# TensorE multiplies the identity until the first rows come, and turns W itself in place of loading its transpose

## The chip, the cores and the metric

The kernel runs on one core of one Trainium2 chip. The metric is the device time of one launch in microseconds (us). One profiled execution is shown beside the timed runs: its span (first to last instruction) and its own time are given below. Engines are named as in the profile: PE is TensorE's matmul, PEld its weight load, DVE VectorE, ACT ScalarE, POOL GpSimd, SP SyncE, which issues most transfers.

## What is computed

A perceiver block in float32: cross-attention of 8 x 64 rows of `x` over 1601 context rows per batch, a linear-attention block with a feed-forward part, and a mixture of 8 experts. Only the first stage concerns the change:

```python
# x: (8, 64, 512), context: (8, 1601, 512), W: (512, 512), b: (512)
p       = layernorm(x)                        # rows of the queries
trans_q = einsum('bqh,oh->bqo', context, W) + b
scores  = einsum('bph,bqh->bpq', p, trans_q)
att     = softmax(scores)
vec     = einsum('bpq,bqh->bph', att, context)
x       = x + relu(einsum('bph,oh->bpo', vec, W) + b)
# then the linear attention with its feed-forward part, then the experts
```

`W` is used twice. The kernel multiplies `W` into the 512 rows of `p` rather than into the context, which contracts over `W`'s first axis; the output projection contracts over its second axis and so needs `W` transposed.

## The kernel before

Every engine's instructions run in the order in which the source writes them. The 512 rows are four tiles of 128 (`t` = 0 to 3, two batches each), and the 512 channels are four blocks of 128 (`KC`).

*Head.* SP issues the loads of `x` (L101, two transfers) and of `W` (L113, tile `w_sb`). GpSimd clears five stretches of `v_sb` (L122) into which the bias row and the last context rows will be loaded, then builds the identity (`make_identity`), then `eps` and further constants. VectorE and ScalarE compute the layer norm of two tiles at a time (L352 to L363). TensorE transposes each tile (`turn_p`, L370) by products with the identity, ScalarE copies the result to `p_t` (tile `h_t`, L371), and `pw_half` (L380) multiplies `W` into it: two halves of 256 rows, four channel blocks each. The order is rows 0 and 1, two blocks of the first half, rows 2 and 3, the rest. ScalarE copies each result to `pw_t` (L387). VectorE then spreads the bias over the partitions (L407) and forms `pb` (L411), which ScalarE adds to the scores as it copies them (L450).

*Cross-attention.* `key_group(t, g)` multiplies `pw_t` by a quarter of the transposed context of two batches (L442, two tiles `ctxT` of 0.8 MB). `softmax` and `turn_scores` (L475) follow, and `weigh(t, g)` (L503) multiplies the weights by the context rows (two tiles `ctx` of 1 MB for each of three groups). `turn_av` and `attended` (L530, L537) apply the output projection with `w_t`, the transposed `W`. These steps are interleaved over the tiles: the key groups of tile 0, two of tile 1, and then in each round one tile's weighing with the next tiles' key groups.

*Transfers.* `stream` writes down one list of loads, and `issue_to` issues them on SP in that order. Context tiles and later weights share a ring of twelve tiles (`RING`); an issue waits until the oldest tile in it has been given back by `done`. The transposed `W` stands in this list behind the first row group of tile 0 (`xw_t`, L197), outside the ring. Each issue also waits for the transfer eight places earlier.

*PSUM.* There are two kinds of banks with four buffers each, `mm` and `acc`. Transposes and the product with `W` use `mm`; scores, weighted sums and outputs use `acc`.

After the cross-attention come the linear attention (from 127 us on), the feed-forward part and the experts (from about 410 us), which the change does not touch.

Of the kernel before, what the change touches and what calls it, by code (L numbers as in the profile page):

```python
# [20 lines left out]
P = 128  # L21
# [3 lines left out]
KC = D // P  # L25
# [15 lines left out]
NBIG = 7  # L41
LN_EPS = 1e-5
RING = 12
AHEAD = 6


@with_exitstack
def perceiver_kernel(
# [5 lines left out]
    context_tail: bass.AP,  # L54
    context_last: bass.AP,
    xw: bass.AP,
    xw_t: bass.AP,
    xb: bass.AP,
    wq: bass.AP,
    wk: bass.AP,  # L60
# [11 lines left out]
    nc = tc.nc  # L72
    const = ctx.enter_context(tc.tile_pool(name="const", bufs=1))
    resid = ctx.enter_context(tc.tile_pool(name="resid", bufs=1))
    ring = ctx.enter_context(tc.tile_pool(name="ring", bufs=RING))
    tails = ctx.enter_context(tc.tile_pool(name="tails", bufs=2))
# [7 lines left out]
    def mm_bank(name):  # L84
        return ps.tile([P, 512], F32, tag="mm", name=name)
# [26 lines left out]
    w_sb = xa.tile([P, KC, D], F32, tag="w", name="w_sb")  # L112
    nc.sync.dma_start(w_sb, xw)  # L113
    w_t = xa.tile([P, KC, D], F32, name="w_t")
# [3 lines left out]
    half = H * DH // 2  # L118
    last_in = [v_sb[:, 2, :half], v_sb[:, 2, half:], v_sb[:, 3, half:], v_sb[:, 1, half:]]
    xb_in = v_sb[:, 0, :D]  # L120
    for rows in [xb_in, *last_in]:
        nc.gpsimd.memset(rows, 0.0)  # L122
    col = const.tile([P, COLS], F32, name="col")

    streamed, order, issued = {}, [], [0]
# [2 lines left out]
    def stream(key, src):  # L128
        order.append((key, src))

    def stream_keys(t, g):
        if t < NT:
            for h in range(2):
                src = context_t[2 * t + h, D * SW * g : D * (SW * g + WIDTHS[g])]
                stream(("ctxT", t, g, h), src.rearrange("(p c k) -> p c k", p=P, c=KC))

    def stream_rows(t, g):
        for h in range(2):
            src = context[2 * t + h, g * GK : (g + 1) * GK, :]
            stream(("ctx", t, g, h), src.rearrange("(p c) d -> p c d", c=GK // P))  # L140
# [9 lines left out]
        stream_keys(1, g)  # L150
    for t in range(NT):
        stream_rows(t, 0)
        if t == 0:
            stream("xw_t", xw_t)
        stream_keys(t + 1, 2)
        stream_rows(t, 1)
        stream_keys(t + 1, 3)
        stream_rows(t, 2)
        stream(("tail", t), context_tail[t])
        for g in range(2):  # L160
            stream_keys(t + 2, g)
        if t == NT - 2:
            for n in range(2):
                stream(("wv", n), wv[n])
# [13 lines left out]
                stream(("e_wo", e, q // 2), e_wo[e, q // 2])  # L178
    place = {key: i for i, (key, _) in enumerate(order)}

    places_of = {"xb": xb_in[0:P:32, :], "col": col, "xw_t": w_t}
    places_of.update({("last", t): last_in[t][0:P:32, :] for t in range(NT)})

    def in_ring(key):
        return key[0] not in places_of and key not in places_of and key[0] != "tail"

    def issue_to(n):

        while issued[0] < min(n, len(order)):
            key, src = order[issued[0]]  # L190
            if in_ring(key) and len(held) >= RING:
                if held[0] not in freed:
                    return
                held.pop(0)
            if key in places_of:
                t_ = places_of[key]
                nc.sync.dma_start(t_, src)  # L197
            elif key[0] == "tail":
                t_ = tails.tile([P, D], F32, tag="tail", name="_".join(str(k) for k in key))
                nc.sync.dma_start(t_, src)  # L200
            else:
                width = WIDTHS[key[2]] if key[0] == "ctxT" else 512
                t_ = ring.tile([P, 4, width], F32, tag="ring", name="_".join(str(k) for k in key))
                nc.sync.dma_start(t_, src)
                held.append(key)
            streamed[key] = t_
            issued[0] += 1

    def done(*keys):

        freed.update(keys)

    def need(*key):
        if key[0] not in ("ctxT", "ctx", "tail", "wv"):
            done(*[k for k in held if place[k] < place[key] - AHEAD + 1])
            issue_to(place[key] + 1 + AHEAD)
        else:
# [3 lines left out]

    ident = const.tile([P, P], F32, name="ident")
    make_identity(nc, ident)
    eps = const.tile([P, 1], F32, name="eps")
    nc.gpsimd.memset(eps, LN_EPS)
    warm0 = const.tile([P, 1], F32, name="warm0")
# [123 lines left out]
    def statistics(src, name):  # L350
        st = small.tile([P, 6], F32, tag="st", name=f"st_{name}")
        nc.vector.bn_stats(st, src)  # L352
        mv = small.tile([P, 2], F32, tag="mv1", name=f"mv_{name}")
        nc.vector.bn_aggr(mv, st)
        std = small.tile([P, 1], F32, tag="std1", name=f"std_{name}")
        nc.scalar.activation(std, mv[:, 1:2], AF.Sqrt, bias=eps)
        return mv, std

    def normalize(dst, src, mv, std, name):

        rstd = small.tile([P, 1], F32, tag="rstd1", name=f"rstd_{name}")
        nc.vector.reciprocal(rstd, std)
        nc.vector.tensor_scalar(dst, src, mv[:, 0:1], rstd, ALU.subtract, ALU.mult)  # L363
# [3 lines left out]
    def turn_p(t):  # L367
        bank = mm_bank(f"tr_p_{t}")
        for c in range(KC):
            nc.tensor.transpose(bank[:, c * P : (c + 1) * P], pn[:, t, c * P : (c + 1) * P], ident)  # L370
        nc.scalar.copy(p_t[:, :, t * P : (t + 1) * P], bank.rearrange("p (c q) -> p c q", c=KC))  # L371
# [4 lines left out]
    def pw_half(half, hc):  # L376
        cols = slice(half * 2 * P, (half + 1) * 2 * P)
        bank = mm_bank(f"pw_{half}_{hc}")
        for oc in range(KC):
            nc.tensor.matmul(  # L380
                bank[:, : 2 * P],
                w_sb[:, oc, hc * P : (hc + 1) * P],
                p_t[:, oc, cols],
                start=(oc == 0),
                stop=(oc == KC - 1),
            )
        nc.scalar.copy(pw_t[:, hc, cols], bank[:, : 2 * P])  # L387
# [3 lines left out]
    for t in range(0, NT, 2):  # L391
        of = [statistics(xs[:, t + h, :], f"p_{t + h}") for h in range(2)]
        for h in range(2):
            normalize(pn[:, t + h, :], xs[:, t + h, :], *of[h], f"p_{t + h}")
        if t == 0:
            turn_p(0)
            turn_p(1)
    pw_half(0, 0)
    pw_half(0, 1)
    turn_p(2)  # L400
    turn_p(3)
    pw_half(0, 2)
# [652 lines left out]
    t = NT - 1  # L1055
# [583 lines left out]
    "ctx_tail",  # L1639
    "ctx_last",  # L1640
    "L0_xattn_W",
    "L0_xattn_W_T",
    "L0_xattn_b",
    "L0_attn_wq",
    "L0_attn_wk",
# [82 lines left out]
```

## Time and profile before

| | us |
|---|---|
| median of 3 timed runs | 650.71 (650.0 to 650.8) |
| the profiled execution, its own time | 647.66 |
| its span | 645.5 |
| TensorE busy in the span | 620.4 (96%) |
| first transpose of rows starts | 7.45 |
| first product with W starts | 10.06 |
| first scores product starts | 27.95 |
| load of the transposed W issued | 31.75 |
| first use of the transposed W | 70.8 |

The page shows the span in 40 slices of 16.1 us; a digit is a busy share in tenths. In the chain of waits, a line holds the start, the duration and what the end of the span was waiting for at that time. In a timeline, a line holds start, duration, engine, source line, operation, output and inputs, the shape and the count; in brackets stand the idle time before it and what ended it. In a table by stretches, the columns are the stretch, its length, the busy time and count of PE, PEld, DVE, ACT and POOL, then granted clock, share of the transfer engines, and GB/s.

### The profile page before, as it was taken

Reading aid. Unit: us, or ns where it says so; the run is one execution under the profiler, and the core shown is the slowest. Engines: PE = TensorE matmul, PEld = TensorE weight load, DVE = VectorE, ACT = ScalarE, POOL = GpSimd, SP = SyncE. Lnnn points to the kernel's source line nnn. Section 1 sums busy time; section 2 is a strip of 40 time slices with the busy share of each in tenths; the row PEclk is TensorE's granted clock in tenths of the full one; section 3 lists DMA queues with packets and bytes.
Section 4 is the critical chain, followed back from the end, with each engine's and each line's share of the span. In section 5 each row is a group of like instructions: output and inputs, shape, how many; then the busy total and the mean of one; then the engine's idle time right before and its main releaser. Section 6 shows DMA issues by size and latency. Waiting matters only on the chain.

```text
span 645.5 us, 7558 instructions
## 1 busy us (share of the span) xinstructions
PE 620.4 (96%) x2956; PEld 292.7 (45%) x2956; DVE 185.5 (29%) x450; ACT 127.8 (20%) x245; POOL 64.6 (10%) x87
## 2 busy tenths in 40 slices
PE   4999999999999999999999999999999999999994
PEld 3743434344444444455444447544443344444441
DVE  5011333332316888660000035511311211011100
ACT  2241222220132123031101211311111111111110
POOL 4000000000000000050000002250102012103000
PEclk9999999999999999999999999999999999999998
DMA  8999999999421203030312222339392549496611
GB/s 345 405 414 422 423 425 421 427 426 422 193 80 47 86 2 131 1 131 0 130 52 79 70 96 95 134 95 348 114 375 54 200 206 338 173 367 188 274 18 16
DMA packets 23755, 132.70 MB, mean 206 GB/s; under 512 B 4084, under 2 KB 4084, under 8 KB 12184
## 3 DMA queue, kind: packets, MB, share of 16 engines
q1 hardware_dynamic: 19352, 123.37, 48.0%
q0 software_dynamic: 3248, 7.58, 5.3%
q10 hardware_dynamic: 1104, 1.07, 0.5%
q8 instruction: 33, 0.54, 0.3%
q14 instruction: 18, 0.15, 0.1%
HBM read 127.10 MB, written 4.91 MB: 204 GB/s over the span
## 4 chain that ended last, share of the span: by engine, by line
PE 50%; DMA 23%; issue 22%; DVE 2%; POOL 1%; POOLq 1%; ACT 0%; SPq 0%; ACTq 0%
DMA out_dram<-y_sb,dst_late 11%; DMA ctx<-in_ctx_dram 11%; PE hid L839 8%; PE mlp L860 8%; PE wk L647 4%; PE wq L647 4%; PE v L567 4%; PE wo L758 4%; PE sc L442 3%; PE av L503 3%; PE pw L380 3%; PE pr_wq L663 1%; PE xo L537 1%; PE qk L689 1%; POOL xg L1166 1%
## 5 line engine op out<-in xcount | busy, mean ns | idle before, releaser
L1243 PE MATMUL up<-e_up,xgT 128*128 128x512 f32 x224 | 100.2, 595 | 2.3 <-PEq L1569 1.4
L1243 PEld LDWEIGHTS up<-e_up,xgT 128*128 128x128 f32 x224 | 40.9, 190 | 49.9 <-issue 48.1
L1251 PE MATMUL y<-e_wo,hidT 128*128 128x512 f32 x128 | 60.8, 598 | 0.0
L839 PE MATMUL hid<-v_sb,w 128*128 128x512 f32 (+2 forms) x144 | 56.6, 545 | 0.0
L1202 DVE TENSOR_TENSOR mid<-up,act 128x256 f32<-128x256 f32 x35 | 14.9, 425 | 132.0 <-ACT act L1200 132.0
L860 PE MATMUL mlp<-w,hid_sb 128*128 128x512 f32 x112 | 51.0, 597 | 0.0
L503 PE MATMUL av<-ctx,eT 128*64 128x512 f32 x192 | 46.6, 597 | 0.7 <-DMA ctx<-in_ctx_dram 0.6
L442 PE MATMUL sc<-ctxT,pw_t 128*64 128x401 f32 (+1 forms) x256 | 46.2, 501 | 0.0
L839 PEld LDWEIGHTS hid<-v_sb,w 128*128 128x128 f32 x144 | 26.2, 190 | 29.1 <-issue 27.3
L1224 POOL DMA_INDIRECT out_dram<-y_sb,dst_late x12 | 18.3, 1524 | 174.3 <-ACT y_sb L1223 55.7
L1200 ACT ACTIVATE act<-up 128x256 f32<-128x256 f32 x35 | 13.4, 384 | 107.2 <-PE up L1243 97.4
L854 POOL TENSOR_TENSOR xin<-xin,b_bc 128x512 f32<-128x512 f32 x4 | 5.1, 1265 | 272.6 <-DVE rstd_h L796 268.4
L1251 PEld LDWEIGHTS y<-e_wo,hidT 128*128 128x128 f32 x128 | 22.5, 190 | 19.9 <-issue 19.6
L860 PEld LDWEIGHTS mlp<-w,hid_sb 128*128 128x128 f32 x112 | 20.7, 190 | 23.5 <-issue 23.4
L442 PEld LDWEIGHTS sc<-ctxT,pw_t 128*64 128x64 f32 x256 | 19.5, 136 | 25.6 <-issue 24.3
L758 PE MATMUL wo<-wo,a_t 128*128 128x512 f32 x64 | 29.1, 600 | 0.5 <-DVE a_t L734 0.5
L647 PE MATMUL wk<-h_t,wk 128*128 128x512 f32 x64 | 29.5, 604 | 0.0
L647 PE MATMUL wq<-h_t,wq 128*128 128x512 f32 x64 | 29.4, 602 | 0.0
L567 PE MATMUL v<-wv,h_t 128*128 128x512 f32 x64 | 28.7, 596 | 0.6 <-DVE h_t L554 0.6
L908 DVE TENSOR_TENSOR xs<-mlp,xs 128x512 f32<-128x512 f32 x3 | 2.1, 692 | 86.6 <-PE mlp L860 86.6
L732 DVE RECIPROCAL rden<-rden 128x512 f32<-128x512 f32 x8 | 26.8, 3353 | 0.3
L503 PEld LDWEIGHTS av<-ctx,eT 128*64 128x64 f32 x192 | 13.7, 136 | 26.8 <-issue 23.2
(266 smaller groups left out, 651.4 us busy)
## 6 DMA issues: line engine op xcount, KB each, us to landing
e_up<-in_L_ffn_up_dram SPq DMA_DIRECT2D x32, 1024.0 KB, 8.0
ctx<-in_ctx_dram SPq DMA_DIRECT2D x24, 1024.0 KB, 17.2
ctxT<-in_ctx_T_dram SPq DMA_DIRECT2D x24, 802.0 KB, 14.8
e_wo<-in_L_ffn_wo_dram SPq DMA_DIRECT2D x16, 1024.0 KB, 9.6
w<-in_L_attn_w_dram SPq DMA_DIRECT2D x8, 1024.0 KB, 4.7
ctxT<-in_ctx_T_dram SPq DMA_DIRECT2D x8, 796.0 KB, 17.5
wv<-in_L_attn_wv_dram SPq DMA_DIRECT2D x2, 1024.0 KB, 16.6
wq<-in_L_attn_wq_dram SPq DMA_DIRECT2D x2, 1024.0 KB, 17.8
```

The source lines that it names most:

```text
L380: nc.tensor.matmul(bank[:, : 2 * P], w_sb[:, oc, hc * P : (hc + 1) * P], p_t[:, oc, cols], start=(oc == 0), stop=(oc == KC - 1),)
L442: nc.tensor.matmul(sc[h * S : (h + 1) * S, :width], pw_t[:, c, (2 * t + h) * S : (2 * t + h + 1) * S], keys[h][:, c, :], start=(c == 0), s ...
L503: nc.tensor.matmul(av[h * S : (h + 1) * S, :], e_t[:, 4 * g + j, h * S : (h + 1) * S], rows[h][:, j, :], start=(g == 0 and j == 0), stop=F ...
L567: nc.tensor.matmul(bank, h_t[:, c, t * P : (t + 1) * P], wv_n[:, c, :], start=(c == 0), stop=(c == KC - 1))
L647: nc.tensor.matmul(bank, w[:, c, (j % 4) * P : (j % 4 + 1) * P], h_t[:, c, :], start=(c == 0), stop=(c == KC - 1),)
L732: nc.vector.reciprocal(rden, rden)
L758: nc.tensor.matmul(wo_banks[t], a_t[:, j, t * P : (t + 1) * P], wo_r[j // 4][:, j % 4, :], start=(j == 0), stop=(j == nj - 1),)
L839: nc.tensor.matmul(hid_banks[f][:, tokens], w[:, c, (f % 4) * P : (f % 4 + 1) * P], h2_t[:, c, tokens], start=(c == 0), stop=(c == KC - 1),)
L860: nc.tensor.matmul(acc[t], hid[:, t * P : (t + 1) * P], need("w2", f // 4)[:, f % 4, :], start=(f == 0), stop=(f == FF // P - 1),)
L1224: nc.gpsimd.indirect_dma_start(out=out, out_offset=bass.IndirectOffsetOnAxis(ap=dst[:n, :], axis=0), in_=y_sb[:n, :], in_offset=None, boun ...
L1243: nc.tensor.matmul(bank, xg_t[c], up_of[q][:, c, :], start=(c == 0), stop=(c == KC - 1))
L1251: nc.tensor.matmul(y, h_t[:, j, :], w[:, 2 * (q % 2) + j, :], start=(q + j == 0), stop=(q + j == NQ))
```

## The change

Twelve products of the identity with itself are written on TensorE right behind the making of the identity, into a bank that nothing reads; the five clears of GpSimd move behind the identity. The load of the transposed `W` and its input go. In its place TensorE transposes the sixteen 128 x 128 blocks of `w_sb` between the transposes of rows 0 and 1 and the product with `W`, into four `acc` banks, and VectorE copies these to `w_t` behind the layer norm of the rows.

```diff
+NIDLE = 12
...
-    for rows in [xb_in, *last_in]:
-        nc.gpsimd.memset(rows, 0.0)
...
     for t in range(NT):
         stream_rows(t, 0)
-        if t == 0:
-            stream("xw_t", xw_t)
         stream_keys(t + 1, 2)
...
     ident = const.tile([P, P], F32, name="ident")
     make_identity(nc, ident)
+
+    idle_bank = acc_bank("idle")
+    for _ in range(NIDLE):
+        nc.tensor.matmul(idle_bank[:, :P], ident, ident, start=True, stop=True)
+    for rows in [xb_in, *last_in]:
+        nc.gpsimd.memset(rows, 0.0)
     eps = const.tile([P, 1], F32, name="eps")
...
         if t == 0:
             turn_p(0)
             turn_p(1)
+
+            w_banks = [acc_bank(f"w_t_{hc}") for hc in range(KC)]
+            for hc in range(KC):
+                for oc in range(KC):
+                    nc.tensor.transpose(
+                        w_banks[hc][:, oc * P : (oc + 1) * P], w_sb[:, oc, hc * P : (hc + 1) * P], ident
+                    )
     pw_half(0, 0)
     pw_half(0, 1)
+    for hc in range(KC):
+        nc.vector.tensor_copy(w_t[:, hc, :], w_banks[hc])
     turn_p(2)
     turn_p(3)
...
-    inputs["L0_xattn_W_T"] = _np.asarray(inputs["L0_xattn_W"]).T
```

## The prediction

> **What bounds the kernel now.** I read the page's busy rows and slices first, then the chain of waits, then the first 180 us engine by engine.
>
> ```profile
> PE 620.4 (96%) x2956; PEld 292.7 (45%) x2956; DVE 185.5 (29%) x450; ACT 127.8 (20%) x245; POOL 64.6 (10%) x87
> PE   4999999999999999999999999999999999999994
> DMA  8999999999421203030312222339392549496611
> ```
>
> TensorE works from the first slice to the last. In the first ten slices (0 to 161 us, the cross-attention) the transfers are at their limit too, at some 0.42 MB per us. Both engines are full there, so one must ask which is late at each place. The chain in order of time says it:
>
> ```profile
> 7.45 1.95 PE tr_p L370 x8
> ...
> 10.06 6.72 PE pw L380 x16
> 16.78 0.87 PE tr_p L370 x8
> 17.65 10.36 PE pw L380 x48
> 28.02 13.68 PE sc L442 x80
> ...
> 42.09 17.31 DMA ctx<-in_ctx_dram
> ```
>
> To 42 us it is TensorE. Then three times (59.40, 87.9/90.3 and 121.2 us) it goes through the landing of a context tile. TensorE's own timeline gives the size of these three waits. The first sixteen products of the third row group of token tile 0 need 4.80 us; without a wait they need 3.65 us:
>
> ```profile
> 58.29 4.80 PE L503 MATMUL av<-ctx,eT 128*64 128x512 f32 x16
> 76.00 3.65 PE L503 MATMUL av<-ctx,eT 128*64 128x512 f32 x16
> 90.34 3.65 PE L503 MATMUL av<-ctx,eT 128*64 128x512 f32 x14 [0.29 <-DMA ctx<-in_ctx_dram]
> 121.25 3.65 PE L503 MATMUL av<-ctx,eT 128*64 128x512 f32 x14 [0.29 <-DMA ctx<-in_ctx_dram]
> ```
>
> The first wait is 4.80 - 3.65 = 1.15 us. At the other two, two records starting at 89.03 and 119.94 us need 0.45 us and the next ones start 1.31 us later: 0.85 us each (part of it is booked as busy). Together TensorE waits 2.85 us for transfers before 121.25 us. After that no single wait of TensorE is over 1.0 us to the end of the span, and none is for a transfer: what is gained at 121.25 us stays.
>
> The two sides are tied at one place. The ring of twelve tiles is full at 25.8 us, and the next transfer is issued only when the first scores product has given its tiles back, at 30.89 us. By then the transfers have nearly run dry:
>
> ```profile
> 30.89 0.80 SPq L204 DMA_DIRECT2D ctx<-in_ctx_dram  x2
> 31.00:32.00 1.00, 1.00 (x8) 0.43 (x6) 0.00 (x0) 0.54 (x1) 0.00 (x0) 1.00 1.14 376
> 32.00:33.00 1.00, 1.00 (x8) 0.43 (x6) 0.00 (x0) 0.00 (x0) 0.00 (x0) 1.00 0.84 232
> ```
>
> The last column is GB/s, about 420 elsewhere: (44 + 188 + 14) / 420 = 0.6 us of transfer time are lost from 31 to 34 us.
>
> **The change, part by part.** *The load of W's transpose goes.* It is 1024 KB at 31.75 us, ahead of all but two of the context's row tiles: 1.049 MB / 0.422 MB per us = 2.48 us. Every later landing comes that much earlier if SP issues in time.
>
> *The first products at half speed.* Sixteen records of the W product take 6.72 us, forty-eight take 10.36: 0.427 us from start to start against 0.216. The starts change pace at 15.9 us. (The profile's granted-clock column says 1.00 throughout; only the starts show it.) So 10.06 to 15.9 us costs 5.84 / 2 = 2.9 us. Thirty-two products in the code give 64 records, while a transpose gives one. The twelve products of the identity are hence 24 records of 128 columns. A transpose of that width starts every 0.214 us at half speed (eight in 1.95 us with a wait between, five in 1.30) and every 0.109 at full speed (eight in 0.87); a record of a product has the same rate per column (256 columns 0.427). They run 24 x 0.214 = 5.1 us.
>
> *When they can start.* Before, GpSimd clears five tiles first (2.37 us) and the identity is ready at 3.70 us. Moved ahead, it is ready near 1.37 us, so TensorE works from about 1.45 to 6.6 us, ends 0.85 us ahead of the first normalized rows (7.45 us), and delays nothing. The clears now end at 3.8 us. Behind them on GpSimd stands eps, needed by ScalarE's square root at 5.91 us; on SP the bias load (3.61 us) may wait 0.3 us, and the key loads behind it come while 3.7 MB are under way. No cost.
>
> *The sixteen transposes of W*, between the transposes of the rows and the W product. At full speed: rows 0 to 7.9 us, rows 1 from 8.05 (normalized at 8.02) to 8.5, W landed at 1.74 + 7.1 = 8.84, so 16 x 0.109 = 1.74 takes them to 10.6. ScalarE's two copies (0.59 each) end at 9.2 beneath them, and the gap of 0.68 us that TensorE had is filled. Then 16 x 0.216 = 3.45, 0.87, 48 x 0.216 = 10.36: the scores start at 25.3 us in place of 28.0, TensorE 2.7 us ahead. At half speed: 16 x 0.214 = 3.43, and the W product starts at 12.6 us.
>
> *Four copies of 512 columns out of PSUM on VectorE*: nearest row, the copy of avT at 0.69 us; 2.8 us, from 11.7 to about 14.5. Behind them on VectorE stand the bias shuffle and pb (3.3 us), done near 18.5 instead of 15.9; the first reader is ScalarE's scores copy, at 28 us or later. The scores reuse the banks, free at 14.5. w_t is first read at 70.8 us. No cost, as long as the scores don't start before 18.5.
>
> *Does the pace rise?* The row: it rose at 15.9 us, 5.8 us after the first product and 8.4 us after the first transpose. [...]
>
> **The sum.** If TensorE is 0.6 us or more ahead at the first scores, the dip at 31 to 34 us goes as well, and the landings move by 2.48 + 0.6 = 3.1 us. TensorE itself could move by 2.85 + 2.7 = 5.5 us. The smaller counts: 3.1 us at 121.25 us, and I take 3.0. From the profiled span: 645.5 - 3.0 = 642.5 us, its own time 647.66 - 3.0 = 644.7. The shown runs lie 3 us above the profiled one; the difference carries over: 650.7 - 3.0 = 647.7 us. Note what the sum says: most of TensorE's lead comes back as longer waits for context, and the removed load is worth more than the faster clock.
>
> **The rivals.** [...]
>
> *The load was hidden anyway.* Then only TensorE's lead would count and the waits at the three places would not shrink or move; gain 0 to 0.4, time 650.5. Against it: the transfers are full from 4 to 166 us and three waits end in a landing.
>
> *The head turns into the bound (slower).* One mechanism: W's transposes at half speed push the W product to 12.6 us, and full speed comes late. Break-even is where half the slow time equals 0.38 + 2.48, that is full speed at 18.3 us; from 20.9 us on it is slower by more than 1.3 us. At 23 us the scores start 4.8 us late, the transfers stand idle meanwhile, and the time is 650.7 + 4.8 - 2.5 = 653.0. Against it: no stretch of the trace is slow for more than 8.4 us after TensorE's start.
>
> **How the numbers follow.** Forecast 0.70 (its own range 646.8 to 648.6), pace stays low 0.18, load hidden 0.05, head as bound 0.07. 0.2% of the time, 1.3 us, is about what a measurement of this kernel can tell from no change. Faster: 0.70 and a little of the second, 0.72; same: the rest of the second and the third, 0.21; slower 0.07. Likeliest 647.7; the range reaches from 646.6 (a lead that also spares the small dips at 23 to 25 us, and the runs' spread of 0.4) to 650.5, well into the second case.
>
> **What would show it.** W-product starts 0.216 us apart from the first; identity records from 1.5 to 6.6 us; first scores near 25.3 us; no dip at 31 to 34 us; the landing at 121.25 us now near 118.2, with TensorE's three waits no shorter than before. Wrong would be: starts 0.427 us apart after 12.6 us, scores later than 28 us, or landings at 59.4, 90.3 and 121.2 us that have not moved.

## The result and the profile after

The changed kernel takes 648.17 us (median of 11 runs, 646.47 to 649.68) beside 650.62 us before (11 runs). The ratio is 0.9955, 95% interval 0.9941 to 0.9969: faster by 0.45%, 2.9 us (2.0 to 3.8); the two medians lie 2.45 us apart. Five of the eleven runs took 646.5 to 647.4 us at a mean granted clock of 0.996, and six took 648.2 to 649.7 us at 0.993; the profiled execution (span 645.1 us, own time 646.8 us) is one of the five.

Busy rows and slices of the page, after:

```profile
PE 623.1 (97%) x2996; PEld 296.0 (46%) x2996; DVE 187.7 (29%) x454; ACT 128.0 (20%) x245; POOL 64.6 (10%) x87
PE   8999999999999999999999999999999999998994
DMA  8999999999411103030311323249382749497511
```

TensorE has 40 records more (24 products of the identity, 16 transposes) and is busy in the first slice. The rest looks as before, which is why the head must be read instruction by instruction. TensorE's timeline after:

```profile
1.45 4.55 PE L223 MATMUL idle<-ident 128*128 128x128 f32 x24 [1.45 <-POOL ident masks.py:199]
7.25 1.38 PE L372 MATMUL tr_p<-ident,xin 128*128 128x128 f32 x8 [1.25 <-DVE xin L365]
8.91 1.96 PE L404 MATMUL w_t<-ident,w_sb 128*128 128x128 f32 x16 [0.29 <-DMA w_sb<-in_L_xattn_W_dram]
10.71 3.62 PE L382 MATMUL pw<-h_t,w_sb 128*128 128x256 f32 x16
...
57.23 3.65 PE L514 MATMUL av<-ctx,eT 128*64 128x512 f32 x14 [0.37 <-DMA ctx<-in_ctx_dram]
88.26 3.65 PE L514 MATMUL av<-ctx,eT 128*64 128x512 f32 x14 [0.38 <-DMA ctx<-in_ctx_dram]
119.12 3.65 PE L514 MATMUL av<-ctx,eT 128*64 128x512 f32 x14 [0.25 <-DMA ctx<-in_ctx_dram]
```

The 24 records need 4.55 us where 5.1 was worked out for half speed throughout; their starts change pace at about 4.8 us. The first sixteen records with W need 3.62 us in place of 6.72. The three waits for context are still there, 2.2, 2.1 and 2.1 us earlier than before (59.44, 90.34, 121.25).

The head in the chain of waits after, where the load of W has become its first link:

```profile
1.74 7.12 DMA w_sb<-in_L_xattn_W_dram
...
8.91 1.96 PE w_t L404 x16
10.87 3.46 PE pw L382 x16
14.33 0.87 PE tr_p L372 x8
15.21 10.36 PE pw L382 x48
25.57 10.98 PE sc L453 x64
...
36.94 15.38 DMA ctxT<-in_ctx_T_dram
```

TensorE reaches the scores 2.45 us earlier (25.50 in place of 27.95), and from 36.5 us on the chain follows transfers; before, it left TensorE only at 41.7 us. The dip of 31 to 34 us is gone, but a longer one has come. By stretches of a microsecond, last column GB/s, after:

```profile
23.00:24.00 1.00, 1.00 (x6) 0.87 (x6) 0.00 (x0) 0.12 (x1) 0.00 (x0) 1.00 1.02 351
...
26.00:27.00 1.00, 1.00 (x10) 0.42 (x8) 0.00 (x0) 0.00 (x0) 0.00 (x0) 1.00 0.94 309
...
28.00:29.00 1.00, 1.00 (x10) 0.42 (x8) 0.00 (x0) 0.51 (x1) 0.00 (x0) 1.00 1.00 263
...
31.00:32.00 1.00, 1.00 (x10) 0.42 (x8) 0.00 (x0) 0.60 (x1) 0.00 (x0) 1.00 1.01 411
```

Against 420, the eight stretches from 23 to 31 us (351, 352, 367, 309, 385, 263, 359, 391) lack 583 KB, 1.4 us of transfer time. The share of the transfer engines stays at 0.94 to 1.03 in these stretches, so they are not idle; their packets take longer, and the profile does not say why. The kernel before lost 0.3 us at 23 to 25 (377 and 329 GB/s) and 0.6 us at 31 to 34 us.

### The profile page after: what moved, and what is told of

Same layout as the page of the kernel before. It is cut to its first block, busy times and chain, and to the rows that moved or that the text cites. A ratio compares the mean times of both kernels' runs of the same rounds, so it can differ in the third digit from the quotient of the medians.

```text
span 645.1 us, 7643 instructions
## 1 busy us (share of the span) xinstructions
PE 623.1 (97%) x2996; PEld 296.0 (46%) x2996; DVE 187.7 (29%) x454; ACT 128.0 (20%) x245; POOL 64.6 (10%) x87
## 4 chain that ended last, share of the span: by engine, by line
PE 47%; DMA 25%; issue 22%; DVE 2%; POOL 1%; POOLq 1%; ACT 0%; SPq 0%; ACTq 0%
DMA out_dram<-y_sb,dst_late 11%; DMA ctx<-in_ctx_dram 10%; PE hid L850 8%; PE mlp L871 8%; PE wk L658 4%; PE wq L658 4%; PE v L578 4%; PE wo L769 4%; DMA ctxT<-in_ctx_T_dram 2%; PE av L514 2%; PE pw L382 2%; PE sc L453 2%; PE pr_wq L674 1%; DMA w_sb<-in_L_xattn_W_dram 1%; PE xo L548 1%
## 6 DMA issues: line engine op xcount, KB each, us to landing
ctxT<-in_ctx_T_dram SPq DMA_DIRECT2D x8, 796.0 KB, 16.5
```

## Experiments

My theory: up to 121 us the landings of context set the time; the removed load makes them earlier, and TensorE's faster start is only worth what it prevents. The rival: the faster start is the gain.

**The twelve products alone.** The identity and the products move ahead of the clears as in the change; the load stays and W is not turned.

```diff
     make_identity(nc, ident)
+    idle_bank = acc_bank("idle")
+    for _ in range(NIDLE):
+        nc.tensor.matmul(idle_bank[:, :P], ident, ident, start=True, stop=True)
```

> The twelve products and the moved clears alone; the load of the transposed W stays, W is not turned. My theory (the removed load carries the gain, TensorE's lead comes back as waits for context): TensorE reaches the scores 2.5 to 3.4 us earlier, but the three landings move only by what the dip at 31 to 34 us gives back, 0 to 0.6 us; 0 to 0.6 us faster than before. Rival (the faster start carries the gain): 2 to 3 us faster, all of the change's gain.

Measured: 650.50 us (13 runs) beside 650.49; ratio 1.0003 (0.9991 to 1.0015). TensorE's timeline of this kernel:

```profile
9.43 3.72 PE L385 MATMUL pw<-h_t,w_sb 128*128 128x256 f32 x16 [0.68 <-ACT h_t L376]
...
24.32 5.96 PE L447 MATMUL sc<-ctxT,pw_t 128*64 128x401 f32 x34
...
57.57 1.04 PE L508 MATMUL av<-ctx,eT 128*64 128x512 f32 x2
59.94 3.65 PE L508 MATMUL av<-ctx,eT 128*64 128x512 f32 x14 [1.32 <-DMA ctx<-in_ctx_dram]
...
121.99 3.22 PE L508 MATMUL av<-ctx,eT 128*64 128x512 f32 x13 [0.26 <-DMA ctx<-in_ctx_dram]
```

The scores start 3.6 us earlier and every product with W runs at full speed, but the third row group of tile 0 goes on at 59.94 us (59.44 before) and that of tile 2 at 121.99 us (121.25). The whole lead is waited away by 60 us. The theory holds, the rival falls. The 0.6 us that I allowed from the dip did not come either: the dip moved here too, to 23 to 32 us (282 to 398 GB/s, 1.5 us against 420, where the kernel before lost 0.9), and TensorE goes on 0.7 us later at tile 2.

**The change without the products.**

```diff
-    idle_bank = acc_bank("idle")
-    for _ in range(NIDLE):
-        nc.tensor.matmul(idle_bank[:, :P], ident, ident, start=True, stop=True)
```

> The change without the twelve products: the load goes, W is turned on TensorE at whatever pace it has. If transposes do not count for the pace: the W product starts at 12.6 us at half speed, the scores 1.3 to 3.0 us later than in the kernel before, and the time is +0.5 to -1.2 us against before. If they count: full pace at 11 to 14 us, scores at 26 to 27 us, 2 to 3 us faster than before.

Measured: 648.83 us (10 runs), ratio 0.9974 (0.9955 to 0.9992), about 1.7 us faster. TensorE's timeline:

```profile
7.28 1.94 PE L368 MATMUL tr_p<-ident,xin 128*128 128x128 f32 x8 [7.28 <-DVE rstd_p L360]
9.08 3.67 PE L400 MATMUL w_t<-ident,w_sb 128*128 128x128 f32 x16
12.55 3.69 PE L378 MATMUL pw<-h_t,w_sb 128*128 128x256 f32 x16
16.07 1.04 PE L368 MATMUL tr_p<-ident,xin 128*128 128x128 f32 x8
...
27.40 2.92 PE L449 MATMUL sc<-ctxT,pw_t 128*64 128x401 f32 x16
...
120.49 3.65 PE L510 MATMUL av<-ctx,eT 128*64 128x512 f32 x14 [0.26 <-DMA ctx<-in_ctx_dram]
```

Up to 12.55 us TensorE has done nothing but 24 transposes, at half speed (16 in 3.67 us; after the products, 1.96). Then sixteen records with W need 3.69 us, full speed. In this execution the pace rose behind transposes alone, some 5.3 us after the first of them (7.28 us), as in the expectation's second reading. The scores start at 27.40 us, later than the 26 to 27 expected, and the gain is below the 2 to 3 us expected of that reading: TensorE passes the third place only 0.76 us early (120.49). The next run shows that the late scores are not the reason.

**The load removed and nothing put in its place.** VectorE copies W as it is, without turning it.

```diff
-        if t == 0:
-            stream("xw_t", xw_t)
...
     pw_half(0, 1)
+    for hc in range(KC):
+        nc.vector.tensor_copy(w_t[:, hc, :], w_sb[:, hc, :])
```

> The load of the transposed W goes and nothing takes its place on TensorE: VectorE copies W untransposed, so the turning is left out of the computation and the experts are chosen differently, which makes the time after 400 us no measure; only the stretch up to 180 us is read. My theory: the head is as before, the landings at 59.4, 90.3 and 121.2 us move by up to 2.5 us, and TensorE is 2.1 to 2.5 us early at 121 us. Rival (the load was hidden): TensorE is less than 0.5 us early there.

TensorE's timeline up to 121 us:

```profile
27.43 2.92 PE L442 MATMUL sc<-ctxT,pw_t 128*64 128x401 f32 x16
...
118.44 3.65 PE L503 MATMUL av<-ctx,eT 128*64 128x512 f32 x14 [0.24 <-DMA ctx<-in_ctx_dram]
```

118.44 is 2.8 us ahead of 121.25: the 2.48 us of the load, and some 0.25 us of a smaller dip (393, 340, 401 and 401 GB/s at 31 to 35 us). The head was only 0.5 us faster than before. The load is worth all of its transfer time, without any help of the clock. The total (650.92 us) says nothing, since other experts are chosen.

The run without the products, above, reaches the scores at the same time (27.40 us) and has moved as many bytes by 118 us (48.31 MB, 48.35 MB here), yet it goes on at tile 2 some 2 us later. The landing records of the two traces tell why. Each tile has sixteen of them, one for each transfer engine. The tile awaited at this place was in on fourteen engines by 118.23 us there and 118.27 us here, but on the last at 120.45 and 118.40 us, and TensorE went on only then, at 120.49 and 118.44 us. So it is one lagging transfer engine that takes that run's gain, and not TensorE's lateness. The lag grew in two steps, to 1.6 us at 28.5 us and 3.3 us at 52.0 us, each just after a fetch of 16 KB of instructions (25.08 and 49.06 us). That the fetches made it was not tried.

**Eighteen products in place of twelve.**

```diff
-NIDLE = 12
+NIDLE = 18
```

> The change with eighteen products of the identity in place of twelve, so that TensorE works until the first rows come (36 records, to about 7 us). The runs of the changed kernel lie in two groups, 646.5 to 647.4 us at a mean granted clock of 0.996 and 648.2 to 649.7 at 0.993. If the second group is a fall back to half speed in the 4.7 us from the last product of the identity to the first product with W (transposes not counting as work), the shorter stretch of 3.6 us makes it rare: runs at 0.996, median about 1 us lower than the change. If it is something else, both groups stay.

Measured: 646.85 us (5 runs, 646.24 to 647.92), ratio 0.9946 (0.9933 to 0.9960). One run of the five was at a mean granted clock of 0.993, so that group became rarer but did not go. The products end at 8.26 us and the transposes of the rows start at 8.09 us, 0.84 us later than with twelve; the scores start at 25.58 us all the same (25.50), since the transposes of W start at 8.99 us, and with twelve they had waited for their load until 8.91 us.

**The turning moved behind the key groups of tile 0.**

```diff
     for g in range(4):
         key_group(0, g)
+    for hc in range(KC):
+        bank = mm_bank(f"w_t_{hc}")
+        for oc in range(KC):
+            nc.tensor.transpose(bank[:, oc * P : (oc + 1) * P], w_sb[:, oc, hc * P : (hc + 1) * P], ident)
+        nc.vector.tensor_copy(w_t[:, hc, :], bank)
```

> The change with the sixteen transposes of W moved from the head to between the key groups of tile 0 and of tile 1 (banks of the other kind). Theory (the landings set the time up to 121 us, TensorE has time to spare): the scores start 1.3 to 1.8 us earlier than in the change, the landings do not move by more than 0.3 us, the time is that of the change within 0.5 us. Rival (the head's length counts): 1 to 1.8 us faster.

Measured: 647.18 us (6 runs), ratio 0.9946 (0.9931 to 0.9960); the changed kernel beside it 647.49 us. TensorE's timeline:

```profile
24.21 11.00 PE L444 MATMUL sc<-ctxT,pw_t 128*64 128x401 f32 x64
...
119.29 3.65 PE L505 MATMUL av<-ctx,eT 128*64 128x512 f32 x14 [0.26 <-DMA ctx<-in_ctx_dram]
```

The scores start 1.29 us earlier than in the change, and the landing of tile 2 lets TensorE go on at 119.29 us (119.12 and 118.74 in two profiles of the change). The head's length does not count; with full speed from the start, the place of the turning is free.

**The five small loads moved.** This asks where the new dip comes from. SP waits for the transfer eight places back; from 13 to 19 us five of the eight are loads of 8 to 32 KB, so few large ones are under way. The issues of the next key tiles in SP's timeline of the kernel before:

```profile
20.86 4.94 SPq L204 DMA_DIRECT2D ctxT<-in_ctx_T_dram  x4
```

The same in the changed kernel:

```profile
22.40 4.84 SPq L200 DMA_DIRECT2D ctxT<-in_ctx_T_dram  x4
```

And with the small loads moved:

```profile
11.01 6.41 SPq L200 DMA_DIRECT2D ctxT<-in_ctx_T_dram  x5
28.60 0.81 SPq L200 DMA_DIRECT2D ctx<-in_ctx_dram  x2
```

```diff
-    for t in range(NT):
-        stream(("last", t), context_last[t])
-    stream("col", columns)
     for g in range(2):
         stream_keys(1, g)
     for t in range(NT):
         stream_rows(t, 0)
+        if t == 0:
+            stream("col", columns)
...
+        stream(("last", t), context_last[t])
         stream(("tail", t), context_tail[t])
```

> The change with the five small loads (four rows of last context, the columns) moved in SP's list: the columns behind the first row group, each last row ahead of its tail. Theory: in the changed kernel the transfers fall to 260 to 390 GB/s from 23 to 31 us since SP, which waits for the transfer eight places back, has five small loads among its eight and issues the next key tiles only at 22.4 us, when the slowest of sixteen engines has landed the tile before (it had fetched 16 KB of TensorE's instructions at 18.7 us); about 1.0 us of transfer time. Then here the key tiles go out by 18 us, the fall goes, and TensorE passes the third row group of tile 2 at about 118.1 us in place of 119.1: 0.7 to 1.0 us faster than the change. Rival (the fall is the fetch itself, or the twelve-tile ring): still a fall, no change of time.

Measured: 646.01 us (5 runs, 645.79 to 647.12), ratio 0.9931 (0.9917 to 0.9944), 1.5 us below the changed kernel's 647.49 us in the same comparison; four of the five runs lie below the lowest of that kernel's five (646.63). Two of the stretches with the small loads moved:

```profile
26.00:27.00 1.00, 1.00 (x8) 0.43 (x6) 0.00 (x0) 0.13 (x1) 0.00 (x0) 1.00 1.00 411
...
28.00:29.00 1.00, 1.00 (x8) 0.43 (x6) 0.00 (x0) 0.35 (x1) 0.00 (x0) 1.00 1.06 436
```

And TensorE's timeline of the same kernel:

```profile
118.17 3.65 PE L514 MATMUL av<-ctx,eT 128*64 128x512 f32 x14 [0.27 <-DMA ctx<-in_ctx_dram]
```

No dip, and tile 2's landing at 118.17 us, as worked out (118.1). The shallow list of transfers is shown as a cause. At tile 2 it is worth 0.6 to 0.9 us (118.74 and 119.12 in the changed kernel); the rest of the 1.5 us is not placed. What seems to make it bite in the changed kernel is a fetch of 16 KB of instructions, which the transfer queues show at 18.7 us after, and at 29.0 us before. The transfer queues of the changed kernel from 18 to 20 us (packets, MB, share of sixteen engines):

```profile
q1 hardware_dynamic: 140, 0.79, 97.7%
q8 instruction: 1, 0.02, 3.4%
```

It takes 1.1 us of one of the sixteen engines. The key tile ahead lands on fifteen of them by 21.0 us and on the last at 22.4 us (20.8 before), and SP waits for the last. That the fetch is this delay fits six profiles with an early fetch (16.9 to 20.1 us, key tiles issued at 22.2 to 22.4: the change three times, the products alone, eighteen products, the late turning) and four with a late one (25.1 to 29.0 us, issued at 20.9 to 21.0); it was argued from these and not tried by itself. By itself the fetch is not the dip: with the small loads moved it comes at 18.7 us too, and one engine lands each tile from 22 to 43 us some 1.6 us after the fourteenth, but the rate does not fall (411 to 449 GB/s from 23 to 33 us).

**Both together.** Small loads moved, eighteen products.

```diff
-NIDLE = 12
+NIDLE = 18
...
+        stream(("last", t), context_last[t])
         stream(("tail", t), context_tail[t])
```

> The moved small loads and eighteen products of the identity together, the candidate for the best version: if both gains hold, the landing of tile 2 at about 118 us, 0.7 to 1.0 us below the kernel with eighteen products alone (646.85), some 646.0.

Measured: 646.20 us (6 runs), ratio 0.9935 (0.9922 to 0.9948), the same as with twelve. So the six further products add nothing here, and the version with the small loads moved and twelve products has the lowest median found.

**The changed kernel again.**

Without an edit, beside the last three.

> The changed kernel once more beside these. If the difference to the kernel with eighteen products was real, its median lies about 1 us above that; if it was chance, within 0.3 us.

Measured: 647.49 us (5 runs), ratio 0.9950 (0.9937 to 0.9963). It lies 0.6 us above the kernel with eighteen products, which ran on another chip, and the two intervals overlap: whether six more products help stays open. Tile 2 goes on at 118.74 us here, 119.12 in the first profile.

**The kernel before, profiled again.**

Without an edit.

> The kernel before, profiled once more. In the profile after, TensorE is 2.1 us early at 433 us and only 0.2 us early at the end; the loss lies in the experts' last token groups, which the change doesn't touch. If the first profile of the kernel before was a fortunate one there, this one shows the same 1.6 to 2 us of waits in those groups and a span near 648.3 us (the median of its runs); if the loss belongs to the change, those groups are as in the first profile and the span is near 645.5.

Its span is 646.5 us. Between 429 and 437 us it loses 1.6 us against the first profile, in two waits of 0.8 us (one for gathered token rows, one with no visible cause), and nothing after that; the waits at 532 and 587 us of the profile after (twice 0.8 us, a product of the experts behind no visible cause) are not in it, but neither are they in the next kernel, which has the changed kernel's instructions. So both readings of the expectation miss: the experts' stage moves by 1 to 2 us from one execution to the next, in other places each time. One pair of profiles cannot measure a change of 3 us to the end of the span; stages can be compared, and totals need many runs.

**The changed kernel with the unread input.**

```diff
     xw: bass.AP,
+    xw_t: bass.AP,
...
     "L0_xattn_W",
+    "L0_xattn_W_T",
```

> The changed kernel with the transposed W still handed over as an input that nothing reads. Time less span is 2.16 us for kernels that have this input and 1.72 us for those without it (medians of their runs). If the input itself costs it, it is 2.1 to 2.2 us here and the time 0.4 us above the change; if not, 1.7 us.

Measured: 644.42 us (13 runs) beside 647.78, ratio 0.9941 (0.9928 to 0.9954); the chip of these runs is some 3 us faster for both. Time less span is 1.71 us, as without the input, and 2.14 for the kernel before beside it. The 0.4 us outside the span does not come from handing over an input that is not read; it goes along with the load. Why is open.

With this profile there are three of the changed kernel's instructions and two of the kernel before. The first product of the experts starts at 406.99, 406.61 and 407.73 us in the three, and at 409.13 and 408.94 us in the two: what TensorE has gained at tile 2 is still there. From that product to TensorE's last, these five executions need 226.6 to 229.5 us.

## Why the prediction was right

*The time.* 647.7 us were forecast from 650.7, 3.0 us faster; measured 648.17 us, 2.9 us faster (interval 2.0 to 3.8). Part of this closeness is luck. 647.7 lies between the two groups of runs, and the median depends on how many of the eleven fell into the group at the lower clock. The profiled execution was forecast at 642.5 us of span and 644.7 us of time and took 645.1 and 646.8: the forecast carried over that the runs lie 3 us above the profiled one, and after the change they lie 1.4 us above it.

*What bounds the kernel.* Right: the landings at the three places set the time up to 121 us. The products alone show it most clearly (a lead of 3.6 us, no gain), and the late turning once more (1.29 us of lead, no gain). The waits there are larger than the forecast read, though, and do not grow as it said. Before:

```profile
119.94 1.02 PE L503 MATMUL av<-ctx,eT 128*64 128x512 f32 x2
...
124.83 1.08 PE L513 MATMUL av<-tail,eT 64*64 64x512 f32 x4
...
146.84 3.65 PE L503 MATMUL av<-ctx,eT 128*64 128x512 f32 x16
150.43 1.08 PE L513 MATMUL av<-tail,eT 64*64 64x512 f32 x4
```

After:

```profile
117.85 1.02 PE L514 MATMUL av<-ctx,eT 128*64 128x512 f32 x2
...
122.70 1.08 PE L524 MATMUL av<-tail,eT 64*64 64x512 f32 x4
```

A third row group takes 150.43 - 146.84 = 3.59 us without a wait and 124.83 - 119.94 = 4.89 us with one, so the second and third waits are 1.3 us each and not 0.85. The three together are 3.7 us before and 4.0 us after. The landings remain the smaller side of the sum, so the forecast time does not change, but only 0.3 us of TensorE's 2.45 us of lead came back as longer waits, where the forecast expected most of it.

*The removed load, 2.48 us.* Right in mechanism and size: 2.8 us at 121 us with the load alone gone, of which 2.48 is the load.

*The first products at full speed.* Right: scores at 25.50 us, forecast 25.3. What the pace is worth is settled only in part. By itself it is worth nothing. Within the change, eighteen products took 646.85 us where none took 648.83 us in the same comparison, four of the five runs below all ten; for twelve, the ratios 0.9955 and 0.9950 stand against 0.9974 without, with intervals that overlap. The forecast let a slow head cost time through late scores (0.38 in its break-even is 10.06 + 2.92 - 12.6 us). In the profile without the products that is not what cost it: the scores were as late with the load alone gone, and 2.8 us were gained there. The difference is the lagging transfer engine. How the products could bear on that, and whether they do in most executions, is open. One step of the arithmetic for that profile is also off: by the expectation's own figures full speed at 11 to 14 us puts the scores at 26.5 to 28.0 us, 1.5 to 0 us early, and not at 26 to 27; the measured 27.40 us lies in that range.

*The step that was mis-sized: "the dip at 31 to 34 us goes as well", + 0.6 us.* The dip went, but 1.4 us were lost from 23 to 31 us instead, 0.5 us more than the 0.9 us that the kernel before lost in both its dips. So the landings moved by 2.48 - 0.5 = 2.0 us, where 3.1 was forecast; at tile 2 three profiles of these instructions show 2.1, 2.5 and 1.4 us against the first profile of the kernel before (119.12, 118.74 and, with the unread input, 119.86), and 0.2 us less against its second (121.06). I had asked what a faster TensorE frees in the ring, and not what else its instructions bring: their fetch came 10 us earlier and fell into the stretch in which SP had few large transfers under way.

*What filled the gap.* 0.44 us lie outside the span (1.72 in place of 2.16 us, medians of the runs), which the sum did not have: it carried the difference of time and span over unchanged. With it, 2.0 + 0.4 = 2.4 us are accounted for of the measured 2.9 (2.0 to 3.8). In the last comparison it is less: 121.06 - 119.86 = 1.2 us at tile 2 and 0.4 outside the span, of 3.8 us (3.0 to 4.7). So 0.5 to 2.2 us are not placed; the profiles show nothing more gained up to the first product of the experts, and behind it single executions differ by up to 2.9 us. That the forecast of 3.0 us fits so closely is partly errors that offset each other.

*When full speed came.* It came 3.4 us after the first product of the identity in the profile after (1.45 to about 4.8 us; 3.2 to 5.7 us in all eight profiles with such products), and some 5.3 us after the first transpose in the run without the products (7.28 to about 12.6 us). No run shows the times for the rise of the pace on which the case "pace stays low" (0.18), the upper end of the range and both readings of the run without the products rest; these two figures are what the runs showed in their place. That case fell: in the run without the products the sixteen records with W from 12.55 us on needed 3.69 us, and the scores started 0.55 us earlier than before (27.40 in place of 27.95 us), not later. The small loads, which the forecast counted only as the dip at 23 to 25 us, were worth 1.5 us.

*No cost for VectorE's copies and GpSimd's clears.* Right: the copies took 10.79 to 13.27 us, pb was ready at 16.5 us, and the scores' first copy on ScalarE came at 28.49 us.

## What to carry to other kernels

Where transfers and TensorE are both full, look for the wait that comes last: a lead of 3.6 us on TensorE was worth nothing, a removed megabyte its full 2.5 us. Work put on TensorE in place of the transfer was free here, since TensorE waits for transfers anyway (4.0 us at the three places): the sixteen transposes took 1.96 us, and the run that turned W later started the scores 1.29 us earlier for no gain. TensorE went on when the slowest of a tile's transfer engines was through (120.45 us in the run without the products, 118.40 us with the load alone gone), though both had moved as many bytes by 118 us (48.31 and 48.35 MB): look at the last engine. Small loads in an ordered list with a fixed look-back use up places that large ones need: moving five of them was worth 1.5 us beside the change's 2.9.

## What the hardware showed that I had not expected

In the run without the products TensorE came to full speed behind transposes of float32 blocks alone: 24 of them from 7.28 us, and full speed from about 12.6 us. A fetch of TensorE's instructions (16 KB, 1.1 us on one transfer engine of sixteen) came just ahead of a tile that landed 1.4 us late on one engine, and through it held up the list behind it; this link is argued from ten profiles. The fetch followed TensorE's pace: it came when 82 to 93 records of TensorE had started, in all twelve profiles, which is at 18.7 us after and 29.0 us before. A lag of one engine stayed for a long time: in the run without the products the last engine was 3.3 us behind the fourteenth at 52.0 us and still 2.2 us behind at 120.45 us. The profile's granted-clock column read 1.00 in every stretch of the head, also where records started at half pace (before, records with W 0.427 us apart from 10.06 to 15.9 us, 0.216 us afterwards).
